# Layer 0 of a two-layer graph network: the weighted sum of a tile grows transposed in PSUM

## The chip, the core and the metric

The kernel runs on one core of one Trainium2 chip. The metric is the device time of one execution in microseconds. A core has five engines, each with its own queue of instructions that it works off in order: TensorE (PE, matrix products and transposes, output only to PSUM), VectorE (DVE), ScalarE (ACT), GpSimd (POOL, which here mostly issues gathers by DMA) and SyncE (SP, which issues DMAs). They wait for one another through semaphores. "PEld" in the profile is the loading of weights into TensorE.

## What is computed

The input is a matrix `x` of 3327 nodes with 512 features each and an adjacency matrix `adj` of zeros and ones, sparse, symmetric, with ones on the diagonal. Both layers end in a residual and a layer normalisation. The change concerns layer 0, a graph attention with four heads:

```python
feats = jnp.einsum('nf,hfo->hno', X, W)
e_s = jnp.einsum('hno,ho->hn', feats, a_self)
e_n = jnp.einsum('hno,ho->hn', feats, a_neigh)
logits = leaky_relu(e_s[:, :, None] + e_n[:, None, :], 0.2)
logits = logits + NEG_INF * (1.0 - A)[None, :, :]
attn = softmax(logits, axis=-1)
out = einsum('hnm,hmo->hno', attn, feats) + b[:, None, :]
out = transpose(out, (1, 0, 2)).reshape(N, 512)
x = layernorm(x + relu(out))
```

Layer 1 is a second gated graph network on the same adjacency. It needs the layer-0 result of every node, gathered by neighbour.

## The kernel before

**Stages.** The nodes are handled in 26 tiles of 128. From the start to about 205 us the kernel builds the feature table `table0` in device memory and turns the adjacency matrix into a list of neighbours for every node. Nodes are sorted by number of neighbours, so that tile j needs only `CAPS[j]` neighbour slots (4 to 14). Two tiles, 0 and 12, hold the nodes with the most neighbours and have one more "stair" slot that is shared out by a small matrix `to_node`. From about 205 to 527 us the kernel works through layer 0, tile by tile in the fixed order 11, 10, 0, 1, 2, ..., 9, 23, 12, 24, 13, 22, 14, 21, 15, 20, 16, 19, 17, 18, 25. From 527 us on it does layer 1. The order of all instructions is written out by hand; each engine's queue follows the order of the program text.

**The ring.** Rows of features arrive in `ring`, 42 slots of one row for each of 128 nodes. `plan` hands out the slots in a circle, tile after tile: the first two slots of a tile hold its nodes' own row of `x` and their own row of features (one gather fetches the pair), then one slot for each neighbour. `gather` puts the gathers into POOL's queue in just that order (L615, one instruction for 128 rows); a gather into a slot waits until the last reader of the old content is done, and all later gathers wait behind it. `finish` raises the count of freed slots (`free`) and calls `gather`, which settles where the gathers stand in the program; when they run is settled by the readers of each slot.

**One tile of layer 0.**

- `weigh_a` and `weigh_b` compute the attention weights of all slots of a tile (DVE, one exponential on ACT). `weigh_a` needs all the tile's rows. It also copies the own row of `x` out of the ring into the tile's result `row1(j)` with ACT (L771).
- `attend` multiplies each slot's row by its weights and adds it up. Slots with s % 3 == 2 are multiplied by ACT (four instructions of 128 columns, L795), the others by DVE (L797). The sum is made on PE: a matmul with the identity as weights and the row of 512 columns as moving operand accumulates into `acc` (L803). The bias is added either by a further matmul (L789, first three tiles) or by DVE onto the first row (L802, "lean" tiles).
- After the third row, PE does `columns2` of the tile two places earlier: a product of the transposed result with eight vectors that layer 1 needs.
- `finish` (L885, DVE) takes the maximum of `acc` with 0 and adds the row of `x` from `row1(j)`. In program order it stands after the `attend` of the *next* tile.
- `columns1` transposes the result on PE, `columns2a` copies it to SBUF with ACT, `columns3` stores the eight columns. Statistics, the normalisation (`publish`, L842) and the writing of the row to `table1` follow. For the last 14 tiles that write is a scatter on POOL (L146), and it is called once all gathers have been put into the queue.
- In the first seven rounds `sort1` also sorts the second group's lists (DVE L551, L553 and PE L557).

The round of the loop numbered i thus puts into the queues: `columns2a` of tile i-2, `attend` of tile i with `columns2` of tile i-2 inside, `finish` and `columns1` of tile i-1, its statistics, `columns3`, `sort1`, and the weights of tile i+1. Here "tile i" means the i-th in the order above.

In layer 1 a sum over neighbours is already made with transposes (`plain_sum`, L1098): the row is the stationary operand in pieces of 128 columns and the identity is the moving one.

Of the kernel before, what the change touches and what calls it, by code (L numbers as in the profile page):

```python
# [8 lines left out]
F32 = mybir.dt.float32  # L9
AF = mybir.ActivationFunctionType  # L10
ALU = mybir.AluOpType
# [3 lines left out]
P = 128  # L15
# [10 lines left out]
CAPS = (14, 12, 11, 10, 9, 9, 8, 8, 7, 6, 6, 5) + (14, 13, 11, 10, 10, 9, 9, 8, 8, 7, 7, 6, 5, 4)  # L26
# [27 lines left out]
def row_bcast(src, n, offset=0):  # L54

    return bass.AP(tensor=src.tensor, offset=src.offset + offset, ap=[[0, P], [1, n]])
# [22 lines left out]
def sparse_pass(  # L79
# [39 lines left out]
    nc = tc.nc  # L119
    N, F = out.shape  # L120
    NP = x.shape[0]
    H, FO = a_self.shape
    KT = F // P
    NT = NP // P
# [4 lines left out]
    T0 = (0, NG[0])  # L129
    B = len(STAIRS)  # L130
# [4 lines left out]
    const = ctx.enter_context(tc.tile_pool(name="const", bufs=1))  # L135
# [22 lines left out]
    srt = [const.tile([P, n, LW], I32, name=f"srt{i}") for i, n in enumerate(NG)]  # L158
    ident = const.tile([P, P], F32, name="ident")
    ones = const.tile([P, P], F32, name="ones")  # L160
    bias0 = const.tile([P, F], F32, name="bias0")
    bias_g = const.tile([P, F], F32, name="bias_g")
    bias8 = const.tile([P, NCOL], F32, name="bias8")
    ovf = const.tile([P, NT, 3], F32, name="ovf")
# [5 lines left out]
    to_node = const.tile([P, P], F32, name="to_node")  # L170
# [13 lines left out]
    def row1(j):  # L184
        g, i = place(j)
        return x1[g][:, i, :]
# [152 lines left out]
    with nc.allow_non_contiguous_dma(reason="four vectors of 512, onto partitions"):  # L339
        for i, w in enumerate((Wa, Wb)):  # L340
            for s in range(2):
                src = w[0:1, s * F : (s + 1) * F].rearrange("o (k p) -> p (o k)", p=P)
                nc.gpsimd.dma_start(v1[:, :, 3 * s + 1 + i], src)
    nc.gpsimd.dma_start(bias0, row_bcast(b0, F))
    nc.gpsimd.dma_start(bias_g, row_bcast(b_g, F))
    nc.gpsimd.dma_start(selves, diag)
    nc.gpsimd.memset(bias8, 0.0)
# [262 lines left out]
    got, stair = {}, {}  # L610
# [49 lines left out]
    def free(j):  # L660

        freed[0] = ends_at[j]
# [71 lines left out]
    order0 = first[-2:][::-1] + first[:-2] + second[-3:-2]  # L734
# [6 lines left out]
    ws, accs, ws2 = {}, {}, {}  # L741

    def weigh_a(j):
        c = slots(j)
        g, i = place(j)
        w = ws[j] = m0.tile([P, S + 1, H], F32, tag="w", name=f"w{j}", bufs=3)
        es = srt[g][:, i : i + 1, S + 2 : S + 2 + H].bitcast(F32)
        for s0, n, buf, o in got[j]:
            nc.vector.tensor_add(w[:, s0 : s0 + n, :], buf[:, o : o + n, F : F + H], es.to_broadcast([P, n, H]))
        if j in T0:  # L750
            logit = m0.tile([P, H], F32, tag="logit", name=f"logit{j}")
            nc.vector.tensor_add(logit, stair[j][:, F : F + H], es2[g])
            small = psx.tile([P, B * H], F32, tag="pcol", name=f"to_nodes{j}", bufs=2)
            nc.vector.tensor_tensor(
                w[:, C0 + 1 :, :], to_nodes(m0, small, f"n{j}", logit),
                no_step.rearrange("p (b o) -> p b o", o=1).to_broadcast([P, B, H]), ALU.add,
            )
        nc.vector.scalar_tensor_tensor(w[:, :c], w[:, :c], 0.2, w[:, :c], ALU.mult, ALU.max)
        mx = m0.tile([P, 1, H], F32, tag="mx", name=f"mx{j}")
        nc.vector.tensor_reduce(mx[:, 0, :], w[:, :c].rearrange("p s h -> p h s"), AX.X, ALU.max)  # L760
        nc.vector.tensor_sub(w[:, :c], w[:, :c], mx.to_broadcast([P, c, H]))  # L761
        nc.scalar.activation(w[:, :c], w[:, :c], AF.Exp)  # L762

        for s0, n, buf, o in got[j]:
            a = max(s0, 1)
            if a == s0 + n:
                continue
            nc.scalar.copy(srt[g][:, i, a : s0 + n], buf[:, o + a - s0 : o + n, F + H])
        if j in T0:
            nc.scalar.copy(ids2[g], stair[j][:, F + H : F + H + 1])  # L770
        nc.scalar.copy(row1(j)[:, 0:F], got[j][0][2][:, 0, 0:F])  # L771

    def weigh_b(j):
        c, w = slots(j), ws[j]
# [5 lines left out]
            small = psx.tile([P, B * H], F32, tag="pcol", name=f"to_rows{j}", bufs=2)  # L780
            ws2[j] = to_rows(m0, small, f"n{j}", w[:, C0 + 1 :, :])

    def attend(j, lean, between):


        w = ws[j]
        acc = accs[j] = ps.tile([P, F], F32, tag="acc", name=f"acc{j}", bufs=2)
        if not lean:
            nc.tensor.matmul(acc, ident, bias0, start=True, stop=False)  # L789
        for s0, n, buf, o in got[j]:  # L790
            for s in range(s0, s0 + n):
                gv = buf[:, o + s - s0, 0:F].rearrange("p (h o) -> p h o", h=H)
                if s % 3 == 2:
                    for h in range(H):
                        nc.scalar.activation(gv[:, h, :], gv[:, h, :], AF.Copy, scale=w[:, s, h : h + 1])  # L795
                else:
                    nc.vector.tensor_tensor(  # L797
                        gv, gv, w[:, s, :].rearrange("p (h o) -> p h o", o=1).to_broadcast([P, H, FO]), ALU.mult
                    )
                row = buf[:, o + s - s0, 0:F]  # L800
                if lean and s == 0:
                    nc.vector.tensor_add(row, row, bias0)  # L802
                nc.tensor.matmul(  # L803
                    acc, ident, row, start=(lean and s == 0), stop=(s == CAPS[j] and j not in T0)
                )
                if s == 2:
                    between()
        if j in T0:
            gv = stair[j][:, 0:F].rearrange("p (h o) -> p h o", h=H)
            nc.vector.tensor_tensor(  # L810
                gv, gv, ws2[j].rearrange("p (h o) -> p h o", o=1).to_broadcast([P, H, FO]), ALU.mult
            )
            nc.tensor.matmul(acc, to_node, stair[j][:, 0:F], start=False, stop=True)

    turned = {}
# [8 lines left out]
    def columns2a(j):  # L826
        xt1s[j] = m0.tile([P, KT, P], F32, tag="xt1", name=f"xt1_{j}")
        nc.scalar.copy(xt1s[j], turned[j])  # L828

    def columns2(j):  # L830
        xt1 = xt1s[j]
        pcol = psx.tile([P, B * H], F32, tag="pcol", name=f"pcol{j}", bufs=2)[:, :NCOL]
        for k in range(KT):
            nc.tensor.matmul(pcol, xt1[:, k, :], v1[:, k, :], start=(k == 0), stop=(k == KT - 1))  # L834
        turned[j] = pcol
# [46 lines left out]

    def finish(j):
        y = row1(j)[:, 0:F]
        nc.vector.scalar_tensor_tensor(y, accs[j], 0.0, y, ALU.max, ALU.add)  # L885
        free(j)
        gather()

# [43 lines left out]
    psx = tc.alloc_tile_pool(name="psx", bufs=1, space=PSUM, side="right")  # L932
    psum = psx.tile([P, B * H], F32, tag="pcol", name="pv1sum", bufs=2)[:, :NCOL]
    for k in range(KT):
        nc.tensor.matmul(psum, ones, v1[:, k, :], start=(k == 0), stop=(k == KT - 1))
    nc.vector.tensor_copy(v1sum, psum)
    norm = Norm(m0, "n0", {3, 7, 11, 15, 19, 22, 24, 25})
    for j in order0[:2]:
        weigh_a(j)
        weigh_b(j)  # L940
    for j in order0[:2]:
        attend(j, False, lambda: None)
    weigh_a(order0[2])
    weigh_b(order0[2])
    for j in order0[:2]:
        finish(j)
    ready = [[], []]
    for i in range(NT + 3):
        for args in ready[0]:
            publish(*args)  # L950
        ready = [ready[1], []]
        third = order0[i - 2] if 2 <= i < NT + 2 else None
        if third is not None:
            columns2a(third)
        if 2 <= i < NT:
            attend(order0[i], i >= 3, lambda: third is None or columns2(third))
        elif third is not None:
            columns2(third)
        if 0 < i <= NT:
            j = order0[i - 1]  # L960
            y = row1(j)[:, 0:F]
            if i > 2:
                finish(j)
            if not waiting:
                put_rows()
            columns1(j)
            done = norm.add(i - 1, y)
            if done:
                k0, scale, shift = done
                ready[1] = [  # L970
                    (order0[k], scale[:, k - k0 : k - k0 + 1], shift[:, k - k0 : k - k0 + 1]) for k in range(k0, i)
                ]
        if i > NT:
            put_rows()
        if 2 <= i < NT + 2:
            columns3(order0[i - 2])
        if 0 < i <= 7:
            sort1(rankis[1], 2 * i - 2, 2 * i)
        if i == 8:
            climb(1, m0, psx.tile([P, B * H], F32, tag="pcol", name="climb1", bufs=2)[:, : B + H])  # L980
        if i == NG[0]:
            nc.vector.memset(over, 0.0)
            for j, c in enumerate(CAPS):
                if j in T0:
                    nc.vector.tensor_scalar(over[:, j, c:S], no_step, 0.0, None, ALU.is_lt)
                else:
                    nc.vector.memset(over[:, j, c:S], 1.0)
        if i == 3:
            nc.sync.dma_start(own1[:, 0, :], xo[N0:])
            nc.sync.dma_start(own1[:, 1, :], singles)  # L990
        if 2 <= i < NT - 1:
            weigh_a(order0[i + 1])
            weigh_b(order0[i + 1])
# [635 lines left out]
```

## Time and profile before

| | us |
|---|---|
| median of 3 runs | 899.11 |
| lowest and highest | 894.95, 904.59 |
| the profiled execution | 897.77 |
| its span, first to last instruction | 895.8 |
| PE busy in the span | 745.3 |
| DVE busy | 693.3 |
| POOL busy | 595.2 |
| ACT busy | 272.0 |
| gathers on POOL (L615), 482 in both layers | 475.7 + 13.9 + 4.2 |
| mean granted TensorE clock | 0.908 of full |

The profile is of one execution. A group of instructions is given as line, engine, operation, output<-inputs and count, then the time in which at least one of them was busy and the mean duration of one in ns, then the idle time of its engine before them. One f32 matmul of the program is two instructions on PE; a transpose is one. In the timeline each piece has its start, its length, and in brackets how long the engine had been idle before and what ended that idle time. Windows give the busy time of each engine in a stretch, with the granted TensorE clock (1.00 is full, 0.50 half).

### The profile page before, as it was taken

To read this page: it belongs to the slowest core of one execution; us is meant where nothing else is said; L and a number is where in the kernel's file an instruction comes from. 1 tells how busy PE (TensorE), PEld (TensorE's weight loads), DVE (VectorE), ACT (ScalarE), POOL (GpSimd) and SP (SyncE) were. 2 spreads that over 40 slices of the span, in tenths; PEclk is the share of its full clock that TensorE was granted. 3 is DMA by queue.
4 is the path that set the end of the run, shared out by engine and by line. 5 is a ranking of instruction groups with operands and counts; after the bars stand their busy time and mean duration, and the time that the engine had idled before them with its cause. 6 is when DMAs were issued, how large, how long until landed. Compare 5 with 4: busy or idle time off the path is not lost. (4 is left out here: it accounts for less than half of the span.)

```text
span 895.8 us, 11378 instructions
## 1 busy us (share of the span) xinstructions
PE 745.3 (83%) x3118; PEld 457.4 (51%) x3118; DVE 693.3 (77%) x2032; ACT 272.0 (30%) x794; POOL 595.2 (66%) x641
## 2 busy tenths in 40 slices
PE   4698997416799978799999957987997999999992
PEld 3477775103445534344444435654764666666551
DVE  4288787896678858769898845957996999998973
ACT  0122221002335525444646512212222222232231
POOL 6711133566577777777777747777777777777772
PEclk9799999556899989889999967999898999999997
DMA  8989999999777878789777637677767777777641
GB/s 330 369 340 403 366 377 345 380 387 399 267 225 227 276 234 263 231 278 329 219 234 228 222 115 203 188 199 201 187 184 196 192 196 195 203 193 199 195 187 74
DMA packets 73352, 224.74 MB, mean 251 GB/s; under 512 B 12736, under 2 KB 16784, under 8 KB 72384
## 3 DMA queue, kind: packets, MB, share of 16 engines
q0 software_dynamic: 46368, 153.69, 56.9%
q1 hardware_dynamic: 24256, 68.13, 19.9%
q10 hardware_dynamic: 2656, 2.10, 0.7%
q8 instruction: 27, 0.44, 0.2%
q14 instruction: 45, 0.37, 0.1%
HBM read 203.02 MB, written 31.51 MB: 262 GB/s over the span
## 5 line engine op out<-in xcount | busy, mean ns | idle before, releaser
L615 POOL DMA_INDIRECT ring<-table,srt x464 | 475.7, 1025 | 162.1 <-issue 56.2
L803 PE MATMUL acc<-ring,ident 128*128 128x512 f32 x504 | 239.4, 619 | 18.9 <-DVE ring L802 12.9
L1085 DVE SCALAR_TENSOR_TENSOR sw<-ring,e,sw 128x512 f32<-128x512 f32 x226 | 169.8, 751 | 10.7 <-ACT sw L1070 4.2
L803 PEld LDWEIGHTS acc<-ring,ident 128*128 128x128 f32 x504 | 94.4, 196 | 130.3 <-issue 74.3
L371 PE MATMUL pf<-w,xc 128*128 128x260 f32 x416 | 102.9, 410 | 13.1 <-DVE w L311 13.1
L1098 PE MATMUL acc<-ident,ring 128*128 128x128 f32 x904 | 108.6, 280 | 6.2 <-DMA ring<-table,srt 6.1
L797 DVE TENSOR_TENSOR ring<-ring,w 128x512 f32<-128x512 f32 x176 | 111.8, 693 | 0.5
L1098 PEld LDWEIGHTS acc<-ident,ring 128*128 128x128 f32 x904 | 103.6, 145 | 8.1 <-DMA ring<-table,srt 8.1
L1118 PE MATMUL po<-wsa,sT 128*128 128x512 f32 x208 | 95.4, 602 | 4.6 <-DVE za L1148 2.3
L371 PEld LDWEIGHTS pf<-w,xc 128*128 128x128 f32 x416 | 84.1, 205 | 29.3 <-DVE w L311 13.8
L1118 PE MATMUL po<-wg,sT 128*128 128x512 f32 x208 | 93.6, 593 | 0.0
L795 ACT ACTIVATE ring<-ring,w 128x128 f32<-128x128 f32 x304 | 91.5, 390 | 0.0
L383 POOL DMA_DIRECT2D table<-row x26 | 14.2, 549 | 85.2 <-ACT st L380 82.6
L1118 PEld LDWEIGHTS po<-wsa,sT 128*128 128x128 f32 x208 | 39.7, 193 | 56.6 <-issue 56.1
L1118 PEld LDWEIGHTS po<-wg,sT 128*128 128x128 f32 x208 | 37.5, 190 | 37.3 <-issue 37.3
L1149 ACT ACTIVATE za<-za 128x512 f32<-128x512 f32 x26 | 16.4, 630 | 127.7 <-DVE za L1148 127.7
L402 PE MATMUL pc<-at,pow 128*32 128x512 bf16 (+1 forms) x182 | 23.3, 413 | 35.3 <-DMA at<-in_adjB 25.4
L762 ACT ACTIVATE w<-w 128x40 f32<-128x40 f32 (+10 forms) x26 | 6.2, 237 | 127.5 <-DVE w L761 127.5
L375 ACT COPY row<-pf 128x512 f32<-128x512 f32 x26 | 15.2, 586 | 95.4 <-PE pf L371 49.7
L834 PEld LDWEIGHTS pcol<-v,xt 128*128 128x128 f32 x208 | 28.7, 201 | 14.5 <-issue 12.1
L828 ACT COPY xt<-x1t 128x512 f32<-128x512 f32 x26 | 15.2, 584 | 62.9 <-PE x1t L822 62.9
L402 PEld LDWEIGHTS <-pow 128*32 128x32 bf16 x182 | 7.3, 97 | 47.9 <-issue 44.8
(252 smaller groups left out, 918.4 us busy)
## 6 DMA issues: line engine op xcount, KB each, us to landing
at<-in_adjB SPq DMA_DIRECT2D x78, 512.0 KB, 11.5
ring<-table,srt POOLq DMA_INDIRECT x464, 3.9
table<-row POOLq DMA_DIRECT2D x26, 260.0 KB, 6.1
xc<-in_xB SPq DMA_DIRECT2D x6, 1024.0 KB, 8.4
own<-in_xo SPq DMA_DIRECT2D x1, 3640.0 KB, 46.5
own<-table SPq DMA_DIRECT2D x1, 3640.0 KB, 55.2
at<-in_adjL SPq DMA_DIRECT2D x13, 256.0 KB, 9.9
table<-in_xo SPq DMA_DIRECT2D x1, 3120.0 KB, 27.2
```

The lines of the kernel that those rows point to most:

```text
L371: nc.tensor.matmul(pf[:, hh, :HC], xc[:, k, o : o + P], w0[:, k, hh, :], start=(k == 0), stop=(k == KT - 1))
L375: nc.scalar.copy(row[:, 0:F].rearrange("p (h o) -> p h o", h=2), pf[:, :, 0 : F // 2])
L402: nc.tensor.matmul(pc[32 * c : 32 * c + 32, : nt * P], pow2[:, s, :], loaded[i, m], start=(s == 0), stop=(m + 1 not in ms or s == 3),)
L615: return nc.gpsimd.indirect_dma_start(out=out_, out_offset=None, in_=table, in_offset=bass.IndirectOffsetOnAxis(ap=ap, axis=0)).ins
L795: nc.scalar.activation(gv[:, h, :], gv[:, h, :], AF.Copy, scale=w[:, s, h : h + 1])
L797: nc.vector.tensor_tensor(gv, gv, w[:, s, :].rearrange("p (h o) -> p h o", o=1).to_broadcast([P, H, FO]), ALU.mult)
L803: nc.tensor.matmul(acc, ident, row, start=(lean and s == 0), stop=(s == CAPS[j] and j not in T0))
L834: nc.tensor.matmul(pcol, xt1[:, k, :], v1[:, k, :], start=(k == 0), stop=(k == KT - 1))
L1085: nc.vector.scalar_tensor_tensor(sw, g[:, i, 0:F], e[:, s : s + 1], sw, ALU.mult, ALU.add)
L1098: nc.tensor.matmul(pl[:, k, :], row[:, k * P : (k + 1) * P], to_node if steps else ident, start=(i + k == 0), stop=(i == len(rows) - 1 and ...
L1118: nc.tensor.matmul(po, sT[:, k, :], wt[:, k, :], start=(k == 0), stop=(k == KT - 1))
L1149: nc.scalar.activation(za, za, AF.Tanh, scale=0.5)
```

## The change

The sum of a tile is kept transposed: `acc` has the features on the partitions, in four blocks of 128 columns of nodes. Each row is turned by four PE transposes that accumulate in PSUM. With the features on partitions the bias is one number for each partition, so ScalarE can add it and take the maximum with 0 in one instruction for each block (`relu`, into the new SBUF tile `hT`, one buffer). PE turns the result back into a new PSUM tile `back` (`turn_back`, one buffer). `finish` then adds the row of `x`, which it reads from the ring, from the slot into which it was gathered; the copy L771 is gone. The bias is loaded as four rows of 128 and turned once. In a round of the loop, `relu` of tile i-1 stands ahead of tile i's `attend`, and `turn_back` of tile i-1 stands beside `columns2`, after the third row.

```diff
-    bias0 = const.tile([P, F], F32, name="bias0")
+    bias0 = const.tile([P, KT], F32, name="bias0")
+    bias_rows = const.tile([KT, P], F32, name="bias_rows")
...
-    nc.gpsimd.dma_start(bias0, row_bcast(b0, F))
+    nc.gpsimd.dma_start(bias_rows, b0)
...
-        nc.scalar.copy(row1(j)[:, 0:F], got[j][0][2][:, 0, 0:F])
...
-    def attend(j, lean, between):
+    def attend(j, between):
...
-        acc = accs[j] = ps.tile([P, F], F32, tag="acc", name=f"acc{j}", bufs=2)
-        if not lean:
-            nc.tensor.matmul(acc, ident, bias0, start=True, stop=False)
+        acc = accs[j] = ps.tile([P, KT, P], F32, tag="acc", name=f"acc{j}", bufs=2)
...
-                if lean and s == 0:
-                    nc.vector.tensor_add(row, row, bias0)
-                nc.tensor.matmul(
-                    acc, ident, row, start=(lean and s == 0), stop=(s == CAPS[j] and j not in T0)
-                )
+                for k in range(KT):
+                    nc.tensor.matmul(
+                        acc[:, k, :], row[:, k * P : (k + 1) * P], ident, start=(s + k == 0),
+                        stop=(s == CAPS[j] and j not in T0 and k == KT - 1), is_transpose=True,
+                    )
...
-            nc.tensor.matmul(acc, to_node, stair[j][:, 0:F], start=False, stop=True)
-
+            for k in range(KT):
+                nc.tensor.matmul(
+                    acc[:, k, :], stair[j][:, k * P : (k + 1) * P], to_node, start=False, stop=(k == KT - 1)
+                )
+
+    cut_off = {}
+
+    def relu(j):
+
+        hT = cut_off[j] = m0.tile([P, KT, P], F32, tag="hT", name=f"hT{j}", bufs=1)
+        for k in range(KT):
+            nc.scalar.activation(hT[:, k, :], accs[j][:, k, :], AF.Relu, bias=bias0[:, k : k + 1])
+
+    def turn_back(j):
+
+        accs[j] = psx.tile([P, F], F32, tag="back", name=f"back{j}")
+        for k in range(KT):
+            nc.tensor.transpose(accs[j][:, k * P : (k + 1) * P], cut_off[j][:, k, :], ident)
...
-        nc.vector.scalar_tensor_tensor(y, accs[j], 0.0, y, ALU.max, ALU.add)
+        nc.vector.tensor_add(y, accs[j], got[j][0][2][:, 0, 0:F])
...
+    psum = psx.tile([P, B * H], F32, tag="pcol", name="bias_columns", bufs=2)[:, :KT]
+    nc.tensor.transpose(psum, bias_rows, ident[:KT, :KT])
+    nc.vector.tensor_copy(bias0, psum)
...
     for j in order0[:2]:
-        attend(j, False, lambda: None)
+        attend(j, lambda: None)
     weigh_a(order0[2])
     weigh_b(order0[2])
     for j in order0[:2]:
+        relu(j)
+        turn_back(j)
         finish(j)
...
+        back = order0[i - 1] if 2 < i <= NT else None
+
+        def between():
+            if third is not None:
+                columns2(third)
+            if back is not None:
+                turn_back(back)
+
+        if back is not None:
+            relu(back)
         if 2 <= i < NT:
-            attend(order0[i], i >= 3, lambda: third is None or columns2(third))
-        elif third is not None:
-            columns2(third)
+            attend(order0[i], between)
+        else:
+            between()
```

## The prediction, made before the result was known

> **What bounds the kernel now.** I read the page's groups first, then busy time by stage, then POOL's timeline.
>
> ```profile
> L615 POOL DMA_INDIRECT ring<-table,srt x464 | 475.7, 1025 | 162.1 <-issue 56.2
> L803 PE MATMUL acc<-ring,ident 128*128 128x512 f32 x504 | 239.4, 619 | 18.9 <-DVE ring L802 12.9
> ...
> L1098 PE MATMUL acc<-ident,ring 128*128 128x128 f32 x904 | 108.6, 280 | 6.2 <-DMA ring<-table,srt 6.1
> ```
>
> The change attacks L803: 252 rows, two instructions each, 239.4 us. The same sum is made in layer 1 with transposes (L1098): 226 rows, four each, 108.6 us. That looks like 100 us to gain. The stages say otherwise (columns: stretch, length, busy PE, PEld, DVE, ACT, POOL, then clock, DMA share, GB/s):
>
> ```profile
> 245.00:300.00 55.00, 55.00 (x168) 27.75 (x167) 44.44 (x118) 25.56 (x77) 42.00 (x43) 1.00 0.81 238
> ...
> 400.00:450.00 50.00, 47.88 (x154) 23.93 (x154) 41.40 (x113) 25.84 (x78) 38.31 (x39) 1.00 0.87 285
> 450.00:500.00 50.00, 49.08 (x155) 23.94 (x154) 42.71 (x120) 27.14 (x81) 37.99 (x40) 1.00 0.77 223
> ```
>
> PE is full, but POOL shows 0.76 in every one of them, and that is full too: in its timeline each gather takes 0.95 us with 0.30 us before it, 0.95/1.25 = 0.76. From 243.92 to 501.42 us POOL issues 199 gathers with no pause over 0.41, 1.29 us each, whatever PE does.
>
> ```profile
> 214.73 0.94 POOL L615 DMA_INDIRECT ring<-table,srt  x1 [0.60 <-issue]
> ...
> 234.30 0.94 POOL L615 DMA_INDIRECT ring<-table,srt  x1 [0.30 <-issue]
> 241.11 2.51 POOL L615 DMA_INDIRECT ring<-table,srt  x1 [5.87 <-DVE ring L797]
> 243.92 1.32 POOL L615 DMA_INDIRECT ring<-table,srt  x1 [0.31 <-issue]
> ```
>
> ```profile
> 501.42 0.95 POOL L615 DMA_INDIRECT ring<-table,srt  x1 [0.30 <-PE acc L803]
> 502.67 1.03 POOL L146 DMA_INDIRECT table<-x1b,srt  x1 [0.30 <-issue]
> ...
> 517.22 0.98 POOL L146 DMA_INDIRECT table<-x1b,srt  x1 [0.30 <-issue]
> 524.82 0.98 POOL L146 DMA_INDIRECT table<-x1b,srt  x1 [6.62 <-DVE x1b L846]
> ```
>
> So layer 0 has three parts: a head with two stops of POOL (214 to 223, 235 to 241), the gather stream, and a tail in which 11 scatters run back to back and the twelfth waits 6.62 us for the last tiles. The chain of waits begins at 527.40, with the landing of the last scatter; all of layer 1 (368 us) follows it and moves as one block. Only head and tail can move the time.
>
> **What decides: who reads the own row last.** Gathers reuse the 42 slots in order, so the first slot of a tile, its own row of x, is the first to be refilled. Today its last reader is the early ACT copy L771. Tile 0:
>
> ```profile
> 230.97 0.61 ACT L771 COPY x1a<-ring 128x512 f32<-128x512 f32 x1
> ```
>
> ```profile
> 254.64 0.69 DVE L885 SCALAR_TENSOR_TENSOR x1a<-acc,x1a 128x512 f32<-128x512 f32 x1 [1.02 <-PE acc L813]
> ```
>
> The copy ends at 231.58, the slot is refilled at 234.30, and `finish` runs at 254.64. With the change `finish` is the last reader: the refill waits for it, and behind it every later gather. I counted slots along POOL's queue: of the own slots reused up to 442 us every one is refilled before its tile's `finish` ends, 0.1 to 21 us early. The change doesn't wait for a resource that is idle; it makes the bound engine wait.
>
> **Head, step by step.** Slot 0 (tile 11) is refilled at 214.73. After the change it waits for `finish(11)`:
> - DVE's nine multiplications of tiles 11 and 10 end at 219.71, as now. PE's 13 rows end at 229.01 now, and DVE waits 9.21 us for the next product, until 229.36. A transposed row costs 0.44 us at full clock (28 instructions in 3.06 us in the chain, so 7 rows) and about 0.86 at half. The clock was half until 219.0; PE is through at 222, and DVE goes on near 222.6, 6.8 us earlier.
> - ACT's exponential and casts take 1.6 us (as 229.36 to 230.97), to 224.2. Then `relu`, four instructions on 128x128 from PSUM. No row shows it. From below: the PSUM copy of 512 columns takes 0.584, one of 4 columns 0.18, so 0.18 + 0.40/4 = 0.28 each, 1.1 in all. From above: L795's 0.39 each, 1.55. Taken 1.2 (L795 starts one every 0.30). To 225.4.
> - `turn_back`, four transposes, 0.44 to 0.87 plus hand-over: 226.5. DVE is free at 225.8. `finish` 0.69 (L797's row for an addition): 227.5. Tile 10 follows, since `hT` and `back` are single, at 229.3.
>
> The refill goes at 227.5 instead of 214.73. Fourteen gathers later (1.29 each, 245.6) comes tile 0's own slot, which waits for `finish(0)`: DVE from 229.3, 2.2 us of statistics and sorting (233.86 to 236.09 now), 6.7 of multiplications, 4.5 until the weights of tile 1 are done, nine multiplications of 0.62, `finish` 0.69: 249.0. `turn_back(0)` is ready by 247. So that gather goes at 249.1, the next at 250.4, the one after at 251.7 instead of 243.92. **The stream starts 7.8 us late.**
>
> **Stream.** Afterwards a refill comes 42 positions after the own row, two tiles fill 18 to 27 of them, so 15 to 24 gathers (19 to 31 us) lie between the last row of the next tile and the refill. `finish` needs 4.8 us of landing (495.17 to 499.97), 2.1 of weights, 5 to 6 of multiplications and 0.7: 13 to 15 us. It fits; 7.8 us of lateness is kept, not increased.
> What else changes lies beside POOL. PE: 252 rows from 0.86 to 0.44, minus 106 us, plus 26 turns of 0.44 and none of the three bias sums (L789, 4.6). DVE: minus 23 additions of 0.69 (15.9). ACT: minus 16.0 (L771), plus 26 times 1.2. None is the bound (ACT 25 of 50 us), so nothing is gained. If that cover went, the new chain would show: sum complete, `relu` 1.2, ACT's third row 1.2, `columns2` 0.95, `turn_back` 0.44, then `finish`; behind the waiting `relu` stand ACT's row multiplications, behind `turn_back` PE's rows from the fourth on. With rows, copies and hand-overs that is 9 to 12 us a tile, POOL gives 12.4. The turned bias (a transpose, a copy) lies in the stop before 214.84; up to 0.5 us without it.
>
> **Tail.** Last gather 509.2, landed 514.0, weights 515.8, publishing 1.2, four multiplications: 519.5. ACT meanwhile publishes three tiles (2.2), copies, does `relu(18)` to 519.2 and the third row to 520.4; PE then row, `columns2`, `turn_back` to 522.2 (half clock 523.5); `finish(18)` ends at 523.1 to 524.4. Then another `columns1`, copy, `relu(25)`, `columns2`, `turn_back`: `finish(25)` starts at 527.8 to 530.4, against 519.38. The rest is unchanged, so the twelfth scatter goes 8.4 to 11 us later than 524.82. POOL alone would be ready at 525.0 and sets nothing. I take 11: PE will be busy about half of the time, and in stretches like that (530 to 546, 155 to 215) the trace grants half the clock.
>
> **Sum.** Profiled execution 897.8 + 11 = 909. The median of the runs shown is 1.3 above that execution, inside their spread.
>
> **A rule against it.** On the clock the trace says this (windows of 1 us, the column before the last two is the clock), while PE did nothing but transposes from 546.43 to 551.7:
>
> ```profile
> 546.00:547.00 1.00, 0.57 (x3) 0.60 (x4) 0.28 (x1) 0.00 (x0) 0.70 (x2) 0.50 0.47 179
> ...
> 550.00:551.00 1.00, 1.00 (x11) 1.00 (x10) 0.96 (x2) 0.75 (x2) 0.69 (x2) 0.95 0.71 212
> ```
>
> Transposes alone brought the clock up within 4 us. The Trainium skill, "TensorE: Matmul & The Clock Gate", Part 4 (PE-mode transpose), says the opposite: that the full clock "doesn't engage for transpose-mode". By that rule the sum would be the rival "half clock" below, near 970; by the row it isn't, and I go by the row.
>
> **Rivals.**
> - *Half clock throughout.* PE needs 10 rows of 0.87, `columns2` 1.9, two turns 1.8 and some 3 us of waiting for `relu` and the third row: 15.4 us a tile against POOL's 12.4, 24 times 3 = 70: 970. For it: PE idles every tile. Against it: the window above. 0.08.
> - *The chain through ACT becomes the bound* on short tiles (4 to 6 multiplications), each 1 to 2 us over POOL's pace, 10 to 20 such tiles: 15 to 35 more, 920 to 940. For: four hand-overs in a row. Against: DVE idles 15 to 19% of the stretches shown, 2 us a tile. 0.12.
> - *Not slower: the earlier PE pays for the wait.* Place: the two stops of POOL at the head, 10 us beyond the usual pause and length (2.9 from 213 to 223, 7.1 at 241.11). If the refill were released about as early as now, the faster PE would take 6 to 10 off the head and the new tail give back 0.6 to 3.2 (8.4 to 11, less 7.8): 888 to 895, from the point at which `finish(11)` comes before 220. Against: it stands behind the weights of tile 0 and `relu`. 0.16.
> - *The forecast*, 0.64, 901 to 920.
>
> **Range and chances.** Runs of this kernel lie 1% apart, about what can be told from no change, so slower means above 908. Of the forecast 0.40 lies above it; with both slow rivals 0.60. Within 1%: the forecast's 0.24 and 0.11 of the third rival, 0.35. Faster by over 1%: 0.05, its end where the slot costs nothing. The range 892 to 928 leaves out the half clock and the outer halves of the other two, some 0.2.
>
> **What would show it.** Right: gathers waiting for `finish`'s line on DVE, the first near 227, one near 249; then a stream at 1.29; the last gather near 509; the twelfth scatter near 535; layer 1 as long as before. PE busy in the layer falling by a third or more with no gain. Wrong: the gather over slot 0 goes before 220; or pauses in the middle of the stream (the ACT chain or the clock); or layer 1 changes its length.

## The result, and the profile after

The changed kernel takes 905.6 us (median; 900.2 to 907.58) where the kernel before takes 897.09 (893.06 to 904.59): a ratio of 1.0079, with a 95% interval of 1.0063 to 1.0095: 7 us slower by the ratio, 8.5 by the medians. Medians are of all runs of a kernel, ratios only of its fast runs (within 1.5% of its fastest), so that on a chip with a wide spread the two can differ. On another chip, in the last experiment, the ratio was 1.0076 (1.0049 to 1.0102).

The profiled execution took 906.87 us with a span of 904.9, 9.1 more than before. Where they lie, by POOL's timeline (start of the instruction, us):

| | before | after | later by |
|---|---|---|---|
| gather that refills slot 0 (tile 11) | 214.73 | 226.72 | 12.0 |
| first gather of the stream | 243.92 | 254.29 | 10.4 |
| last gather of layer 0 | 501.42 | 509.38 | 8.0 |
| eleventh scatter | 517.22 | 525.42 | 8.2 |
| twelfth scatter | 524.82 | 535.20 | 10.4 |
| first gather of layer 1 | 530.94 | 541.32 | 10.4 |
| end of the span | 895.8 | 904.9 | 9.1 |

All of it is there when the stream begins. The stream makes up 2.4, the tail loses 2.2, and layer 1 takes 1.3 less, which no line of the change explains. Of the page's groups, the two that the change is about:

```profile
L616 POOL DMA_INDIRECT ring<-table,srt x464 | 480.9, 1036 | 166.8 <-issue 51.0
L800 PE MATMUL acc<-ident,ring 128*128 128x128 f32 x1008 | 165.4, 328 | 70.0 <-DVE ring L795 64.6
```

The sum is 74 us shorter on PE (239.4 before). The gathers' 480.9 us are 5.2 more than before, and one long gather, shown below, accounts for that. The windows of the stream (stretch, length, busy PE, PEld, DVE, ACT, POOL, clock, DMA share, GB/s):

```profile
245.00:300.00 55.00, 40.47 (x261) 35.62 (x259) 39.45 (x107) 24.97 (x81) 41.90 (x44) 0.81 0.81 244
...
400.00:450.00 50.00, 39.97 (x247) 37.39 (x247) 39.72 (x109) 29.57 (x98) 37.28 (x40) 0.74 0.83 257
450.00:500.00 50.00, 36.64 (x228) 33.59 (x228) 33.70 (x94) 24.05 (x79) 38.11 (x40) 0.75 0.79 230
```

PE went from full to 37 to 40 of 50 us, and POOL's 0.76 is what it was. PE's gain turned into idle time, and the granted clock of these stretches went from 1.00 to between 0.74 and 0.81 (in one round PE idles from 465.1, and from 468 the clock is 0.50). POOL's timeline at the head and in the tail:

```profile
226.72 0.94 POOL L616 DMA_INDIRECT ring<-table,srt  x1 [10.01 <-DVE x1a L899]
...
230.53 7.64 POOL L616 DMA_INDIRECT ring<-table,srt  x1 [0.30 <-issue]
238.48 1.32 POOL L616 DMA_INDIRECT ring<-table,srt  x1 [0.30 <-PE acc L800]
...
251.77 0.96 POOL L616 DMA_INDIRECT ring<-table,srt  x1 [0.30 <-issue]
```

```profile
525.42 0.99 POOL L146 DMA_INDIRECT table<-x1b,srt  x1 [0.30 <-issue]
535.20 0.98 POOL L146 DMA_INDIRECT table<-x1b,srt  x1 [8.79 <-DVE shifted L859]
```

The first line is the refill of slot 0: it waits 10 us for `finish` (L899), the new last reader of the own row. The gather at 230.53 has no wait before it, but takes 7.64 us. The one at 251.77 goes to tile 0's own slot, and it did not have to wait.

### The profile page after: what moved, and what is told of

It is laid out like the page before. It is cut to its first block, busy times and chain, and to the rows that moved or that the text cites. A ratio compares the mean times of both kernels' runs of the same rounds, so it can differ in the third digit from the quotient of the medians.

```text
span 904.9 us, 12619 instructions
## 1 busy us (share of the span) xinstructions
PE 696.2 (77%) x3733; PEld 529.1 (58%) x3733; DVE 678.4 (75%) x2010; ACT 284.1 (31%) x872; POOL 600.1 (66%) x641
## 5 line engine op out<-in xcount | busy, mean ns | idle before, releaser
L616 POOL DMA_INDIRECT ring<-table,srt x464 | 480.9, 1036 | 166.8 <-issue 51.0
L800 PE MATMUL acc<-ident,ring 128*128 128x128 f32 x1008 | 165.4, 328 | 70.0 <-DVE ring L795 64.6
L800 PEld LDWEIGHTS acc<-ident,ring 128*128 128x128 f32 x1008 | 147.5, 172 | 87.0 <-DVE ring L795 73.7
L1127 PE MATMUL acc<-ident,ring 128*128 128x128 f32 x904 | 108.6, 280 | 6.1 <-DMA ring<-table,srt 6.0
L1127 PEld LDWEIGHTS acc<-ident,ring 128*128 128x128 f32 x904 | 103.7, 145 | 8.0 <-DMA ring<-table,srt 8.0
L848 PEld LDWEIGHTS pcol<-v,xt 128*128 128x128 f32 x208 | 36.6, 263 | 2.0 <-ACT xt L842 2.0
L848 PE MATMUL pcol<-v,xt 128*128 128x8 f32 x208 | 34.3, 293 | 1.3 <-ACT xt L842 1.3
```

The lines of the kernel that those rows point to most:

```text
L616: return nc.gpsimd.indirect_dma_start(out=out_, out_offset=None, in_=table, in_offset=bass.IndirectOffsetOnAxis(ap=ap, axis=0)).ins
L800: nc.tensor.matmul(acc[:, k, :], row[:, k * P : (k + 1) * P], ident, start=(s + k == 0), stop=(s == CAPS[j] and j not in T0 and k == KT - ...
L1127: nc.tensor.matmul(pl[:, k, :], row[:, k * P : (k + 1) * P], to_node if steps else ident, start=(i + k == 0), stop=(i == len(rows) - 1 and ...
```

## The experiments

There are two theories. **Own row**: the loss is the slot of the own row, held until `finish`, so that POOL, the bound of layer 0, stops. **Chain and clock**: the loss is what stands between the last row of a tile and its result (maximum, turning back, addition), or the slower clock under the transposes.

The chips differ, and ratios are always against the kernel before on the same chip. On three of them the kernel before takes 1067 to 1079 us, and POOL pauses more than 0.5 us 16 to 24 times between the gathers of layer 1, 38 to 46 us in sum beyond the usual 0.30, in all ten profiles taken there, though no experiment edits layer 1; in the two profiles above there is no such pause. I call these the slower chips. Experiments 1 to 6 all ran on them, while the times that were expected of these are mostly for a chip of 897 us. They tell directions and places; sizes for the 897 us of the result come from the last experiment, whose chip has that pace (896.5).

**1. The early copy put back.** The changed kernel, with slot 0 read early again:

```diff
 weigh_a:
+        nc.scalar.copy(row1(j)[:, 0:F], got[j][0][2][:, 0, 0:F])
 finish:
-        nc.vector.tensor_add(y, accs[j], got[j][0][2][:, 0, 0:F])
+        nc.vector.tensor_add(y, accs[j], y)
```

> The changed kernel with the early ScalarE copy of the own row put back (finish adds it from the tile's result, not from the ring). Theory 'own row': the gather over slot 0 goes near 216 us instead of 226.7, the stream reaches its last gather near 497 to 502 us instead of 509.4, the twelfth scatter goes near 523 instead of 535.2, and the time is 893 to 898 us. Rival 'chain and clock' (the loss comes from relu, turn_back and the half clock in head and tail, not from the slot): the time stays at 903 to 907 us, and only POOL's first stop moves.

> The changed kernel, with ScalarE's early copy of the own row put back (so slot 0 of a tile is read early again) and the last addition of `finish` reading that copy; the sum is still transposed, and the maximum still on ScalarE. Theory 'own row': the 8 us come from slot 0 being held until `finish`, so the gather that opens each tile waits for it; without the hold 893 to 898 us where the kernel before takes 897 (ratio 0.995 to 1.001), no stop of 10 us for DVE x1a in POOL's waits, first gather of the long stream back at 241 to 245. Rival 'chain and clock': the cost is the longer chain sum, maximum, turning back, addition, and the half clock; the copy then only adds ScalarE work: 903 to 907 (ratio 1.007 to 1.011). On an earlier chip, where the kernel before took 1073 us, this kernel had a ratio of 1.026 (1.011 to 1.042), which favours the rival there; on that chip the gathers themselves came with longer pauses.

> The same kernel as the two runs of this experiment before it (early copy of the own row put back, sum still transposed), which fell on chips where the kernel before takes 1067 to 1073 us instead of 897; there its ratio to the kernel before was 1.014 to 1.026. Theory 'own row': on a chip of 897 us, 893 to 898 us (ratio 0.995 to 1.001), since there the gathers' own pace bounds layer 0; on a chip of 1070 us, 1.01 to 1.03 again. Rival 'chain and clock': 903 to 907 us (ratio 1.007 to 1.011) on a chip of 897 us too.

Measured on three slower chips: 1078.29 us, ratio 1.026 (1.011 to 1.042); 1082.94, 1.014 (1.007 to 1.022); 1083.28, 1.020 (1.011 to 1.029). By the medians of all runs the three are 1.004, 1.015 and 1.004: on the first and the third of these chips the runs of the kernel before lie nearly 4% apart, so the size of the loss is uncertain there. That misses the 0.995 to 1.001 of the own-row theory. Whether the number would hold at 897 us stays open, as none of these chips has that pace.

**2. The late row alone.** The kernel before, with the other half of the change only:

```diff
 weigh_a:
-        nc.scalar.copy(row1(j)[:, 0:F], got[j][0][2][:, 0, 0:F])
 finish:
-        nc.vector.scalar_tensor_tensor(y, accs[j], 0.0, y, ALU.max, ALU.add)
+        nc.vector.scalar_tensor_tensor(y, accs[j], 0.0, got[j][0][2][:, 0, 0:F], ALU.max, ALU.add)
```

> The kernel before with one edit: no early copy, finish reads the own row from the ring; the sum stays a matmul of 512 columns. Theory 'own row': POOL stops at the gather over slot 0 until finish(11), near 233 us (214.7 now), the stream starts 8 to 15 us late and the time is 905 to 912 us, at least as slow as the changed kernel although nothing is transposed. Rival 'chain and clock': 896 to 899 us, as before.

> The kernel before, with only the other half of the change: no early copy, the last operation of `finish` reads the own row from the gather's buffer; the sum and its bias are as before, nothing is transposed. Theory 'own row': slower like the changed kernel, 905 to 912 us (ratio 1.008 to 1.017), with a stop of POOL for DVE x1a ahead of the stream. Rival 'chain and clock': 896 to 899 (ratio 0.998 to 1.003), ScalarE 10 us less busy and nothing else.

> The same kernel as the two runs of this experiment before it (the kernel before without the early copy, own row read by `finish` from the gather's buffer; sum as before), whose ratio was 1.063 to 1.069 on chips where the kernel before takes 1067 to 1073 us. Theory 'own row': on a chip of 897 us, 905 to 925 us (ratio 1.008 to 1.03); on a chip of 1070 us 1.06 to 1.07 again. Rival 'chain and clock': 896 to 899 us (ratio 0.998 to 1.003) on a chip of 897 us.

Measured: 1125.17 us, 1.063 (1.040 to 1.087); 1137.69, 1.069 (1.061 to 1.077); 1142.92, 1.078 (1.055 to 1.100); by the medians 1.048, 1.066 and 1.059. That is far above the 1.008 to 1.03 that was expected for a chip of 897 us, and the largest loss of all the kernels, though the sum has not one transpose. POOL's waits in the second of them (what it waited for, us in all, times, the longest):

```profile
POOL ring L615 <- DVE x1a L884: 107.9, 7, 50.4
...
POOL ring L615 <- DVE x1b L884: 59.7, 6, 12.6
```

L884 is `finish`: 168 us of waiting in 13 stops, 147 and 156 us on the other two chips. In experiment 1, on the same three chips, the waits of gathers for `finish` are 2.6, 0 and 2.3 us. So holding the slot makes POOL wait, and the early copy takes those waits away. Experiments 5 and 6 below say the same with the transposed sum: they keep the late row, and on the second chip their gathers wait 101 and 126 us for `finish`, and they take 16 and 20 us more than experiment 1 there, though each has a small edit of its own besides. What experiment 1 loses lies elsewhere, in its run on the second chip for slots that the transposes release and in front of two scatters:

```profile
POOL ring L616 <- PE acc L801: 42.7, 34, 11.1
```

```profile
POOL table L146 <- DVE shifted L860: 38.6, 2, 26.6
```

No profile of the kernel before was taken on a slower chip, so how much of these waits is there without the change is not shown.

**3. Half of the sum.** The kernel before, adding up only every other row (the last one too). The other rows are left out of the result.

```diff
-                nc.tensor.matmul(acc, ident, row, start=..., stop=...)
+                if s % 2 == 0 or s == CAPS[j]:
+                    nc.tensor.matmul(acc, ident, row, start=..., stop=...)
```

> The kernel before, but only every second row (and the last) of a tile is added into the sum: TensorE's work for the sum is halved, about minus 100 us, and the result leaves out the other rows. Theory 'POOL is the bound of layer 0': 888 to 897 us; only POOL's two stops at the head and the last tiles can shrink. Rival 'TensorE is the bound' (it is shown at 95 to 100%): 800 to 850 us.

Measured: 1061.02 us, ratio 1.012 (0.993 to 1.031) on the first of the slower chips, 0.988 by the medians: no gain that can be told, and nothing like the 800 to 850 us of the rival. The sum falls to 290 of 504 instructions, and PE is busy 34 of 50 us and less in the stream. PE's time for the sum does not bound layer 0 there.

**4. The last two tiles summed in the old way.** Experiment 1, with tiles 18 and 25 as before the change (sum of 512 columns, bias by matmuls, maximum and addition in `finish`):

```diff
+    as_before = order0[-2:]
 attend:
+        if j in as_before:
+            for k in range(KT):
+                one = ident[:KT, k : k + 1].to_broadcast([KT, P])
+                nc.tensor.matmul(acc[:, k, :], one, bias_rows, start=(k == 0), stop=False)
...
+                    nc.tensor.matmul(acc.rearrange("p k n -> p (k n)"), ident, row, ...)
 relu, turn_back:
+        if j in as_before:
+            return
 finish:
+        if j in as_before:
+            nc.vector.scalar_tensor_tensor(y, accs[j].rearrange("p k n -> p (k n)"), 0.0, y, ALU.max, ALU.add)
```

> The early copy put back, and the last two tiles (18 and 25) summed in the old way (matmul of 512 columns, maximum on VectorE), all others transposed. If the tail's loss is the chain through relu and turn_back: 2 to 4 us less than with the early copy alone, 889 to 895 us, the twelfth scatter near 519 to 521. If the tail waits for the landing of the last rows: no difference to the early copy alone.

Measured: 1073.88 us, 1.027 (1.016 to 1.038), on the same chip as the first run of experiment 1 (1.026): no gain that the time shows. POOL's timeline shows the part it touches, first in experiment 1, then here:

```profile
629.28 0.98 POOL L146 DMA_INDIRECT table<-x1b,srt  x1 [12.15 <-DVE shifted L860]
```

```profile
634.57 0.98 POOL L146 DMA_INDIRECT table<-x1b,srt  x1 [9.27 <-DVE shifted L874]
```

The stop before the twelfth scatter falls from 12.15 to 9.27 us; in experiment 3, with the old tail throughout, it is 8.59. So the new chain is worth some 3 us in the tail. The rest of the loss on these chips does not lie in the last two tiles, and where it lies is open.

**5. The maximum done twice.** The changed kernel, with 1.13 us more of ScalarE per tile:

```diff
-        for k in range(KT):
+        for k in [*range(KT), *range(KT)]:
             nc.scalar.activation(hT[:, k, :], accs[j][:, k, :], AF.Relu, bias=bias0[:, k : k + 1])
```

> The changed kernel, with ScalarE's four maxima of every tile done twice (the second time over the same result), so 1.13 us more of ScalarE and of the chain per tile, 29 us over 26 tiles. Theory 'gathers bound layer 0': only the places where POOL waits for a `finish` move: the head by 1 to 2 us, the tail by 1 to 2.5 us: 907 to 910 us where the changed kernel takes 905.6 (ratio to the kernel before 1.010 to 1.015). Rival 'ScalarE's chain bounds the rounds': every round grows by 1.1 us: 925 to 936 us.

Measured: 1099.42 us, ratio 1.035 (1.026 to 1.044), on the second of the slower chips; the kernel of experiment 6 took 1102.52 beside it. If every round had grown by 1.1 us, there would be 29 us between them, unless the other's own edit cost as much. So the maximum does not seem to set the rounds; by what it moves the changed kernel itself can't be said, since that was not timed on this chip.

**6. Four operations of the sort moved to the next round.** It asks about the gather of 7.64 us. In three of the profiles the long gather is another one in POOL's order (the 42nd in the changed kernel, the 54th in the kernel before with 2.51 us, the 49th in experiment 7 with 6.88), and each time it ends within 0.01 us of VectorE's last operation for the second tile's statistics (L694, at 238.17 in the changed kernel).

```diff
-        if 0 < i <= 7:
-            sort1(rankis[1], 2 * i - 2, 2 * i)
+        if 2 <= i <= 7:
+            sort1(rankis[1], 2 * i - 2 if i > 2 else 0, 2 * i)
```

> The changed kernel, with the first two steps of the second sort (four VectorE operations) moved from the round of the second tile to the next round, whose steps they join. It asks about the one gather of 7.64 us at 230.53 in the changed kernel (2.51 us in the kernel before). Theory 'VectorE's run': it is long because VectorE works without a break beside it, beginning with those four operations; with them moved it shortens to 1 to 5 us, a long one may appear a round later, and as the next stop is tile 0's `finish` near 248.7, the stream comes at most 3 us earlier: 902 to 906 us. Rival 'the gather's own': it depends on which gather it is, stays at 7 to 8 us, and the time is that of the changed kernel, 905 to 907.

Measured: 1102.52 us, ratio 1.035 (1.025 to 1.044). First the long gather of experiment 5, on the same chip, with the sort where it was; then VectorE's run and POOL beside it here:

```profile
248.50 7.08 POOL L616 DMA_INDIRECT ring<-table,srt  x1 [0.30 <-issue]
```

```profile
246.94 6.26 DVE L795 TENSOR_TENSOR ring<-ring,w 128x512 f32<-128x512 f32 x10
```

```profile
247.03 1.40 POOL L616 DMA_INDIRECT ring<-table,srt  x1 [0.30 <-ACT xt L842]
248.73 0.95 POOL L616 DMA_INDIRECT ring<-table,srt  x1 [0.30 <-issue]
249.98 0.94 POOL L616 DMA_INDIRECT ring<-table,srt  x1 [0.30 <-PE acc L800]
```

The same ten multiplications run without a break, and the gathers beside them take 0.94 to 1.40 us. No gather of the kernel takes 2 us. That the sort's operations ahead of the multiplications make the long gather does not follow, though: in experiment 2 they stand there too, and no gather of its three runs takes 2 us either. On the second chip:

```profile
264.89 0.65 DVE L553 SCALAR_TENSOR_TENSOR spread<-tiles__359,to,st 128x420 f32<-128x420 f32 x1
265.46 6.27 DVE L796 TENSOR_TENSOR ring<-ring,w 128x512 f32<-128x512 f32 x10
```

```profile
265.39 0.96 POOL L615 DMA_INDIRECT ring<-table,srt  x1 [0.30 <-issue]
266.66 0.94 POOL L615 DMA_INDIRECT ring<-table,srt  x1 [0.30 <-issue]
```

What makes the gather long stays open. And the edit saved nothing: the gather over tile 0's slot, which waits for nothing in the changed kernel (251.77 above), here stands for `finish`:

```profile
278.11 0.95 POOL L616 DMA_INDIRECT ring<-table,srt  x1 [15.59 <-DVE x1a L899]
```

Most of that stop is the edit's own doing. Eight operations of the sort now follow one another, and VectorE waits for PE before the fifth:

```profile
267.47 0.29 DVE L552 TENSOR_SCALAR row_is<-columns,to 128x128 f32<-128x128 f32 x1 [11.27 <-PE sorted L558]
```

Without these 11.27 us some 4 us of the stop would be left (an estimate). In experiment 5, behind the long gather, the same gather waits 2.42 us for `finish`.

**7. The changed kernel and its transposed sum without hold and chain, on a chip of 896.5 us.** The second kernel is experiment 1 with `relu` and `turn_back` returning at once. It leaves out the bias, and the sum that it adds is still transposed:

```diff
 relu, turn_back:
+        return
 finish:
-        nc.vector.tensor_add(y, accs[j], y)
+        nc.vector.scalar_tensor_tensor(y, accs[j].rearrange("p k n -> p (k n)"), 0.0, y, ALU.max, ALU.add)
```

> The changed kernel itself, timed beside the kernel before on the kind of chip on which the experiments run (the kernel before takes 1067 to 1079 us there, its gathers pause far more often). On such chips the late own row alone costs a ratio of 1.063 to 1.078, and the transposed sum with its chain alone 1.014 to 1.026. Theory 'the transposed sum shortens the hold': with the sum done sooner, `finish` comes sooner after a tile's last row, so slot 0 is held for less; both together 1.02 to 1.04, with POOL waiting 30 to 90 us for `finish` where the late row alone makes it wait 130 to 170. Rival 'they add': 1.08 to 1.10, POOL waiting as long for `finish` as with the late row alone.

> The kernel with the early copy put back and the transposed sum kept, but without bias, maximum on ScalarE and turning back: `finish` takes the maximum of the still transposed sum with 0 and adds the own row, in the form of the kernel before. It leaves out the bias and the turning back, so what it adds is transposed; the times of layer 1 are not touched by that. It asks what the 1.4 to 2.6 per cent of the early-copy kernel on these chips are. Theory 'chain': they are the maximum, the turning back and the addition after the last row of a tile; without them ratio 0.99 to 1.006, and the stop ahead of the twelfth scatter (26.6 to 27.5 us with the chain) is 20 to 23. Rival 'transposed sum': they are the four transposes a row and TensorE's lower clock; ratio 1.013 to 1.026 again, the stop 25 to 28.

Measured: the changed kernel 904.04 us, 1.0076 (1.0049 to 1.0102); without hold and chain 891.55 us, **0.9923** (0.9891 to 0.9955), faster than the kernel before. The expectations, 1.02 to 1.04 for the changed kernel and a stop of 20 to 23 us for the other, were for a slower chip and were not tested. POOL's timeline of the changed kernel:

```profile
212.02 0.94 POOL L616 DMA_INDIRECT ring<-table,srt  x1 [1.06 <-DMA ring<-table,srt]
226.71 0.94 POOL L616 DMA_INDIRECT ring<-table,srt  x1 [13.74 <-DVE x1a L899]
...
508.82 0.95 POOL L616 DMA_INDIRECT ring<-table,srt  x1 [0.30 <-issue]
...
534.42 0.99 POOL L146 DMA_INDIRECT table<-x1b,srt  x1 [8.51 <-DVE shifted L859]
```

and of the kernel without hold and chain:

```profile
218.22 1.05 POOL L616 DMA_INDIRECT ring<-table,srt  x1 [0.76 <-DMA ring<-table,srt]
219.76 1.32 POOL L616 DMA_INDIRECT ring<-table,srt  x1 [0.49 <-ACT ring L794]
...
500.11 0.94 POOL L616 DMA_INDIRECT ring<-table,srt  x1 [0.30 <-issue]
...
522.18 0.98 POOL L146 DMA_INDIRECT table<-x1b,srt  x1 [5.03 <-DVE shifted L862]
```

The refill of slot 0 (second line) waits 13.74 us in the one and 0.49 in the other, and the last gather starts at 508.82 against 500.11, 8.7 us later, although the second kernel came to the head 6.2 us behind (218.22 against 212.02, a difference that arises before layer 0). Of the 8.7 us, 7.0 are there at the first gather of the stream (254.20 against 247.20); the other 1.7 arise in the stream, and no run shows from what. The stop before the twelfth scatter is 8.51 against 5.03, 3.5 us more. Together, 8.7 + 3.5 = 12.2 of the 12.9 us between the spans (904.0 and 891.1). The mean granted clock is 0.854 and 0.857: the rival's slower clock is in both kernels, and the second of them is faster than the kernel before, whose clock is 0.908. What is left of the rival is the 3.5 us of chain in the tail.

One caution: the kernels differ in hold and chain at once. That the head's 7.0 us, and with less certainty the 8.7, belong to the hold is read from the line that names the wait, and from experiments 1 and 2, where the waits for `finish` come and go with the early copy. It is not a run of its own at this pace. A kernel with early copy and chain would by this sum have a span of 891.1 + 3.5 = 894.6 us, an estimate, against 895.8 before on the first chip: nothing that a measurement would tell. On the slower chips that kernel, experiment 1, was not faster than the kernel before. No version that beats both and computes the whole result was found.

## Why the prediction was right

It gave 909 us from 897.8 + 11. The profiled span grew by 9.1, the medians lie 8.5 apart. Direction, place and cause hold. Of the chances, most lay on "slower by over 1%", and the measured 0.8% is just inside "within 1%": the sum was 2 to 4 us high, and the bound lay in that gap. By its steps:

- **POOL bounds layer 0, PE's gain buys nothing.** Right for the stream: experiment 3, and 74 us of PE that left no trace there. Not quite for the head. In the kernel before, DVE waits 9.21 us for PE at 229.36; after the change 3.11, and without hold and chain the early PE is worth 0.8% in all (that kernel also does without the bias). The third rival priced this at 6 to 10 us, rightly near, and was right that the hold decides whether it shows. The same VectorE operation before and after:

```profile
229.36 0.20 DVE L754 TENSOR_TENSOR w<-to_nodes,no_step 128x40 f32<-128x40 f32 x1 [9.21 <-PE to_nodes L673]
```

```profile
222.45 0.20 DVE L755 TENSOR_TENSOR w<-to_nodes,no_step 128x40 f32<-128x40 f32 x1 [3.11 <-PE to_nodes L674]
```

- **First stop: refill at 227.5.** It came at 226.72. DVE goes on at 222.45 (222.6 predicted), and `relu`, which no row had shown, takes 1.13 us for a tile where 1.2 was taken:

```profile
224.15 1.13 ACT L822 ACTIVATE hT<-acc,bias 128x128 f32<-128x128 f32 x4
```

- **Second stop: the refill of tile 0's slot waits for `finish(0)` until 249.1.** This step failed. `finish(0)` ended at 249.35 (249.0 predicted), but the gather came to its turn only at 251.77, because of the gather of 7.64 us that I had not foreseen. The step "fourteen gathers later (1.29 each, 245.6)" is the one that is wrong; the stream starts 10.4 us late, not 7.8. With a gather of the usual 0.95 us in its place the turn would have come near 245.1 (an estimate), and the stop that I described would have stood there; experiments 5 and 6 show such a stop on a slower chip, in 6 lengthened by its own edit.

```profile
248.67 0.68 DVE L899 TENSOR_TENSOR x1a<-back,ring 128x512 f32<-128x512 f32 x1
```

- **Stream: lateness kept.** No gather waits for `finish` in it, as the sum of 13 to 15 against 19 to 31 us said. It makes up 2.4 us, so the last gather goes at 509.38: the predicted 509.2 was met by two errors that cancel.
- **Tail: twelfth scatter 8.4 to 11 us late.** 10.4. But the working counted two chains after `finish(17)`, and only one lasts. DVE in the tail:

```profile
515.91 0.69 DVE L899 TENSOR_TENSOR x1b<-back,ring 128x512 f32<-128x512 f32 x1 [1.75 <-PE back L828]
...
525.57 0.69 DVE L899 TENSOR_TENSOR x1b<-back,ring 128x512 f32<-128x512 f32 x1 [2.61 <-PE back L828]
...
529.77 0.68 DVE L899 TENSOR_TENSOR x1b<-back,ring 128x512 f32<-128x512 f32 x1
```

  `finish(17)` and `finish(18)` wait for the turning back, 1.75 and 2.61 us. `finish(25)` waits for nothing: between the two DVE works out the scales of a group of statistics, thirteen small operations of 0.2 us, and the second chain hides behind them. So `finish(18)` was later than predicted (it ends at 526.26, not by 524.4), `finish(25)` within its 527.8 to 530.4, and the term came out right by luck.
- **Layer 1 moves as one block.** It was 1.3 us shorter, within what the spread of the runs allows. With the tail it makes the difference between 11 and 9.1.
- **PE's price of a row.** 252 rows at 0.44 would be 111 us; it is 165.4, with the granted clock at 0.74 to 0.81 instead of 1.00 in the stretches shown. It cost nothing, because POOL leaves the room. The rivals that needed it on the path ("half clock", "chain through ACT") did not occur: no pause in the stream, and experiment 5.

## What to carry to other kernels

When a buffer is handed out in a circle, its price is set by its last reader: moving one read of one slot from the beginning of a tile to its end cost the engine that refills the ring 7 to 9 us, by the reading of the last experiment, and together with the longer chain took back more than the faster sum had given. Before giving up a "superfluous" copy, look in the timeline at who refills what it reads, and whether that engine is the bound. And a gain on an engine that is not the bound, even one that shows full as PE did, is worth only what it shortens at the beginning and the end of the stream, here at the first tiles.

## What the runs showed of the hardware

- A gather on POOL can take 7 us with no wait before it, and ends with a VectorE operation to within 0.01 us (experiment 6). In the changed kernel the DMA engines lie nearly idle meanwhile (the second column from the right is their share):

```profile
232.00:238.00 6.00, 6.00 (x36) 5.24 (x35) 5.96 (x11) 3.01 (x11) 6.00 (x1) 0.68 0.04 14
```

  The Trainium skill, "SBUF — State Buffer", section "SBUF: two separate sides", describes such a thing: while VectorE runs an operation in a two-port mode, GpSimd is locked out of the port pair that they share and can't write its descriptors, so the DMA engines wait. The idle DMA engines fit. But the ten multiplications alone, each with two inputs in SBUF, hold up no gather in experiment 6, nor do they in experiment 2 with the sort's operations ahead of them. So whether it is that lock, which operation takes it, and why it lasts over several operations is not shown.
- The same program takes 897 us on some chips and 1067 to 1079 on others, with longer pauses between the gathers; there the late row alone cost 6 to 8%. What makes these chips slower is not shown, and the late row alone was not run at 897 us.
- The same transposes of a tile's sum took 2.78 us for 24 at 461.89, where the granted clock was 1.00, and 2.82 for 12 at 474.01, after 8.89 us without work, where it was 0.50.
